# Accumulating gathers, rows that carry their weight, and another spread of the indexed transfers in a mixture-of-experts stage

## The chip, the core and the metric

The kernel runs on one core of one Trainium2 chip. The metric is the device time of one execution in microseconds. The core has five engines with a program each: PE (TensorE, matrix products into PSUM), DVE (VectorE), ACT (ScalarE), POOL (GpSimd) and SP (SyncE, which here only issues transfers). Engines wait for each other and for transfers by semaphores.

## The reference

The input x has four images of 32 x 128 x 128 in fp32. Each goes through two layers:

```
# layer 0: attention over the 4096 positions of an image folded 2 x 2
q = fold(x)                                  # 128 channels x 4096 positions
energy = q^T q / (norms)                     # in the reference's terms, d_i d_j
x = gamma * softmax(energy) applied to q + x
# layer 1: tokens t = 4096 rows of 128 per image
t = t + linear attention of layernorm(t)     # 8 heads; products collapse into one matrix
u = layernorm(t)
p, e = top 2 of softmax(u @ router_w + router_b), p normalised to sum 1
t = t + p0 * (u @ expert_w[e0] + expert_b[e0]) + p1 * (u @ expert_w[e1] + expert_b[e1])
```

What the change touches is the last line: for each token the results of its two experts are weighted and added.

## The kernel before

**Layer 0** (attend, line 416) runs image by image. One step of it makes one 128 x 512 block of scores: PE writes pe (line 550), ACT takes its exponential into pr (line 553; 531 in the last row of blocks of the last image) and PE multiplies pr with the values into po (line 439). Blocks are made once for the lower triangle; their transposes for the other triangle go by DVE (line 368), SP and DRAM (472, 487) into the tiles F, from which PE makes the share pg (line 374) at least 57 ticks of a clock of work later. There are 584 steps with an exponential in all, 144 an image and 8 more at the end.

**Everything else** is written as generators, which the loop at the end of the kernel advances by a piece each time the clock of work has moved by 10 (PACE), so about one piece a step. Instructions of PE, DVE, ACT and SP are issued in exactly the order in which these generators emit them. POOL's transfers by index and its powers are kept in program order too (pinned, line 158).

- prep (line 281) brings the next image's columns: loads xx, transposes it (ptq, 312), sums squares on DVE (323, 324), takes the power -0.5 on POOL (rn, 163), scales on DVE (qs, 337) and transposes again on PE (ptn, 345).
- layer1 (line 596) starts for an image when 84% of its steps are done, so most of it runs under the next image. close_rows(kc) closes one of four pieces of 8 rows of tokens: it divides (df, 703), adds to T (725), takes statistics (728), and sends them through close_stats to POOL's power (rsa, 163, and nba, 632). normalise (638) then writes xn, and gram_rows (670) adds to the gram matrix. After all four pieces comes matrix (764). Piece 0 of an image waits until the image before it has set "sorted" (line 686).
- attention_rows and route give each token its two experts, first and second, and their weights.
- sorted_experts(h) (line 914) handles one half h of an image's tokens, 16 rows of tiles. Each token gets two places in a list sorted by experts, one per expert. **32 scatters** on POOL (989) write the rows of xn to the DRAM list xs, one tile of 128 rows each. **Loads** (1015) bring the list back two tiles of one expert at a time, PE transposes them (1058) and multiplies with the expert's matrix (1051), DVE copies the product out (1034) and SP stores it in ys (1037). When all are done the second half sets "sorted". **32 gathers** on POOL (1116) then fetch for each tile of tokens the two results into yb; DVE multiplies them by their weights and adds them to acc (**combine**, 1085), which was fetched from t2 (1092), and SP stores four rows of acc to the output (**put**, 1098).

A scatter or gather waits for the latest exponential (exps), so that they are not issued faster than the steps go. Two are emitted a step. The scatters of half 1 wait in the program for those of half 0 ("moved"), the gathers of half 1 for those of half 0 ("gathered"), and those of half 0 for the scatters of half 1.

**The last image** has no image after it. Its close_rows run within its own last steps and after them; its last part (last_parts) does all experts for every token without sorting. Between the loop and last_parts the generators that are left are run to their end one after another, those of the earlier images first:

```
    for steps, _ in steady:
        for _ in steps:
            pass
    closing.last_parts()
```

## Time and profile before

| | us |
|---|---|
| runs | 1700.94, 1698.34, 1698.80 |
| median | 1698.8 |
| the profiled execution's own time | 1704.26 |
| its span | 1702.5 |
| mean granted TensorE clock | 0.993 |

In the table of groups each row is a line, engine and operation, with its count, busy time, mean length in ns, the idle time of the engine just before and what ended it. Groups that the change touches or that stand beside it:

```profile
L1116 POOL DMA_INDIRECT yb<-ys,place x192 | 185.3, 965 | 246.7 <-ACT pr L553 67.9
L989 POOL DMA_INDIRECT xs<-xn,place x192 | 185.8, 968 | 163.0 <-ACT pr L553 86.7
L384 DVE TENSOR_TENSOR o<-o,pg 128x512 f32<-128x512 f32 x110 | 75.4, 685 | 189.5 <-PE pg L374 156.2
L1034 DVE COPY xn<-pys 128x256 f32<-128x256 f32 x60 | 25.4, 424 | 89.2 <-ACT xn L1025 68.7
L1034 DVE COPY result<-pys 128x256 f32<-128x256 f32 (+1 forms) x60 | 24.6, 410 | 87.1 <-ACT xn L1025 57.8
```

The span falls into four images of about 400 us. The indexed transfers of an image run under the next image, so there are three such stages; the last image ends in a stretch of some 110 us without layer 0 beside it.

### The profile page before, as it was taken

The numbers are of one execution on the slowest core, as the hardware profiler recorded it, in microseconds if no ns is written. First come the engines' busy times: TensorE is split into PE (matmuls) and PEld (weight loads), VectorE is DVE, ScalarE is ACT, GpSimd is POOL, SyncE is SP. The second block draws the span as 40 slices with busy tenths as digits, with TensorE's granted clock in tenths as the row PEclk, the third lists the DMA queues.
The fourth block names the chain that finished last, engine by engine and source line by source line (L and its number), as shares of the span: only waits on it lengthen the run. The fifth ranks groups of instructions, "written<-read, shape, count | busy, mean of one in ns | idle before, by whom it ended". The sixth has DMA issues, their size and how long they took to land.

```text
span 1702.5 us, 21925 instructions
## 1 busy us (share of the span) xinstructions
PE 1651.5 (97%) x5458; PEld 876.1 (51%) x5458; DVE 936.7 (55%) x2443; ACT 926.0 (54%) x2893; POOL 511.0 (30%) x553
## 2 busy tenths in 40 slices
PE   8999999999999999999999999999999999998888
PEld 5444444455554555445554455545555455554643
DVE  4433334467485345478478334556748533454787
ACT  3555445466575555446565555545656455544476
POOL 1000000011026425451015642543102642446166
PEclk9999999999999999999999999999999999999999
DMA  4554756754458777875457777886445876876001
GB/s 135 168 177 157 204 173 219 242 190 162 149 173 266 229 239 243 255 225 161 136 179 235 228 248 240 236 258 194 165 141 167 264 228 216 254 243 193 7 12 39
DMA packets 227053, 325.51 MB, mean 191 GB/s; under 512 B 31472, under 2 KB 155504, under 8 KB 212592
## 3 DMA queue, kind: packets, MB, share of 16 engines
q1 hardware_dynamic: 206416, 285.15, 52.3%
q0 software_dynamic: 12288, 25.19, 5.1%
q10 hardware_dynamic: 8224, 13.77, 2.8%
q8 instruction: 46, 0.75, 0.2%
q14 instruction: 79, 0.65, 0.1%
HBM read 153.85 MB, written 175.24 MB: 193 GB/s over the span
## 4 chain that ended last, share of the span: by engine, by line
PE 79%; DVE 8%; DMA 4%; ACT 3%; issue 2%; SPq 2%; POOL 1%; another core or an unknown queue 0%; ACTq 0%; DVEq 0%; POOLq 0%
PE po L439 22%; PE pe L550 22%; PE pg L374 19%; PE pys L1051 3%; PE py L1200 3%; PE pg L395 2%; PE pys L1058 1%; PE pat L796 1%; ACT xn L638 1%; SPq L487 1%; DMA F<-blocks 1%; DVE df L703 1%; PE pgram L670 1%; PE ptq L312 1%; DMA blocks<-F 1%
## 5 line engine op out<-in xcount | busy, mean ns | idle before, releaser
L553 ACT ACTIVATE pr<-pe 128x512 f32<-128x512 f32 (+1 forms) x576 | 322.4, 560 | 552.0 <-PE pe L550 420.6
L439 PE MATMUL po<-pr,qT 128*128 128x512 f32 (+3 forms) x1152 | 551.9, 561 | 6.3 <-ACT o L444 5.6
L550 PE MATMUL pe<-qn,qn 128*128 128x512 f32 x896 | 462.5, 598 | 5.2 <-ACT pr L553 4.9
L374 PE MATMUL pg<-F,qT 128*128 128x512 f32 x880 | 451.1, 594 | 1.3 <-DMA F<-blocks 1.3
L368 DVE STREAM_TRANSPOSE F<-pr 128x512 f32<-128x512 f32 x440 | 305.8, 702 | 165.8 <-ACT pr L553 144.2
L439 PEld LDWEIGHTS po<-pr,qT 128*128 128x128 f32 x1152 | 216.0, 191 | 254.1 <-issue 223.7
L379 ACT ACTIVATE junk<-F 128x512 bf16<-128x512 f32 x440 | 272.9, 620 | 1.4 <-DMA F<-blocks 1.4
L374 PEld LDWEIGHTS pg<-F,qT 128*128 128x128 f32 x880 | 167.5, 191 | 197.2 <-issue 182.4
L1116 POOL DMA_INDIRECT yb<-ys,place x192 | 185.3, 965 | 246.7 <-ACT pr L553 67.9
L989 POOL DMA_INDIRECT xs<-xn,place x192 | 185.8, 968 | 163.0 <-ACT pr L553 86.7
L550 PEld LDWEIGHTS pe<-qn,qn 128*128 128x128 f32 x896 | 154.3, 192 | 114.7 <-issue 98.2
L384 DVE TENSOR_TENSOR o<-o,pg 128x512 f32<-128x512 f32 x110 | 75.4, 685 | 189.5 <-PE pg L374 156.2
L163 POOL TENSOR_TENSOR rn<-ss,neg_half 128x8 f32<-128x8 f32 (+1 forms) x17 | 26.9, 1584 | 332.6 <-DVE ss L324 332.5
L553 ACT ACTIVATION_READ_ACCUMULATOR pr<-pe 128x1 f32 x576 | 112.1, 195 | 0.0
L1025 ACT ACTIVATE xn<-pys 128x256 f32<-128x256 f32 x120 | 45.3, 378 | 109.8 <-PE pys L1058 87.5
L163 POOL TENSOR_TENSOR rsf<-dm_f,neg_half 128x8 f32<-128x8 f32 (+1 forms) x15 | 26.2, 1744 | 233.7 <-DVE sv_f L630 233.7
L1051 PEld LDWEIGHTS pys<-ew_sb,xn 128*128 128x128 f32 x468 | 69.6, 191 | 46.6 <-issue 43.8
L550 PE MATMUL pe<-qn 128*128 128x512 f32 (+3 forms) x256 | 90.4, 435 | 0.7 <-ACT qn L343 0.7
L379 ACT ACTIVATION_READ_ACCUMULATOR junk<-F 128x1 f32 x440 | 84.4, 192 | 0.0
L163 POOL TENSOR_TENSOR rsa<-dm_a,neg_half 128x8 f32<-128x8 f32 x16 | 26.5, 1654 | 186.5 <-DVE sv_a L630 186.2
L1034 DVE COPY xn<-pys 128x256 f32<-128x256 f32 x60 | 25.4, 424 | 89.2 <-ACT xn L1025 68.7
L1034 DVE COPY result<-pys 128x256 f32<-128x256 f32 (+1 forms) x60 | 24.6, 410 | 87.1 <-ACT xn L1025 57.8
(212 smaller groups left out, 1655.4 us busy)
## 6 DMA issues: line engine op xcount, KB each, us to landing
blocks<-F SPq DMA_DIRECT2D x110, 1024.0 KB
F<-blocks SPq DMA_DIRECT2D x220, 192.0 KB
F<-blocks SPq DMA_DIRECT2D x220, 128.0 KB
xn<-xs SPq DMA_DIRECT2D x114, 128.0 KB
F<-blocks SPq DMA_DIRECT2D x220, 64.0 KB
below<-F SPq DMA_DIRECT2D x31, 384.0 KB
out_dram<-acc SPq DMA_DIRECT2D x128, 64.0 KB
xx<-in_x_dram SPq DMA_DIRECT2D x62, 128.0 KB
```

What stands on the lines that cost most here:

```text
L163: pinned(nc.gpsimd.tensor_tensor(dst, src, neg_half.to_broadcast(list(src.shape)), ALU.pow))
L368: f()
L374: nc.tensor.matmul(pg.rearrange("p (a f) -> p a f", a=4), st["qT"][i][:, ib, :], G[:, :, ib], start=(ib == 0), stop=(ib == NJ - 1),)
L379: nc.scalar.activation(junk, G[:, :, ib], AF.Copy, accum_out=st["sums"][:, NJ * i + ib, jc : jc + 1])
L384: nc.vector.tensor_tensor(o, o, pg.rearrange("p (a j c) -> p a j c", a=4, c=S), ALU.add)
L439: nc.tensor.matmul(row["po"][:, lo:hi], qT[blk // NJ][:, blk % NJ, :], w, start=start, stop=(row["left"] == 0))
L550: nc.tensor.matmul(pe[:, c0:], qn[jc][:, ts(j, P)], qn[i][:, c0:], start=True, stop=True)
L553: nc.scalar.activation(pr[:, c0:], pe[:, c0:], AF.Exp, accum_out=sums[:, t, i : i + 1]).ins
L989: inst = nc.gpsimd.indirect_dma_start(xs[h], offset(place[:, i, k : k + 1]), xn[:, k, :], None)
L1051: nc.tensor.matmul(p[:, 2 * P + j * D : 2 * P + j * D + D], bufs[4 + g % 2][:, j, :], weights[:, bass.ds(begins[2 * (g % 2) + j], D)], sta ...
L1116: inst = nc.gpsimd.indirect_dma_start(yb[k // 4][:, i, k % 4, :], None, ys, offset(place[:, i, k : k + 1]))
L1200: nc.tensor.matmul(bank, xn[:, k, :], ew_sb[:, 4 * h : 4 * h + 4, :], start=True, stop=True)
```

## The change

- A row of the list xs is 132 numbers wide instead of 128 (DW = D + 4). Its last four hold the token's weight for that expert. POOL writes the weights into the same columns of xn before each run of 16 scatters; the scatters go through all rows of the half for the first expert and then for the second, instead of alternating. All other uses of xn name its first 128 columns.
- The product is multiplied on DVE by the weight that came with the row, instead of copied, into one of four buffers of the tile "df" (which close_rows uses too). Six buffers instead of four are loaded into.
- The gathers add in fp32 straight into acc, which is fetched first, so yb, combine and its 192 instructions on DVE are gone. In a group of four rows the gathers for the first expert come first, then those for the second, which add to the same bytes.
- The spread over steps: scatters have a free step after every four (for image 2 after every eight). Gathers go one a step for images 0 and 1, and for image 2 two a step with a free step after every four.
- place has two buffers instead of one.

```diff
-    xs = [dram.tile([NT * P, D], F32, tag=f"xs{h}", name=f"xs_{h}", bufs=1) for h in range(2)]
+    xs = [dram.tile([NT * P, DW], F32, tag=f"xs{h}", name=f"xs_{h}", bufs=1) for h in range(2)]
...
-        xn = big1.tile([P, KT, D], F32, tag="xn", name=f"xn_{b}")
+        xn = big1.tile([P, KT, DW], F32, tag="xn", name=f"xn_{b}")
...
-        place = stat.tile([P, 2, KT], U32, tag="place", name=f"place_{b}", bufs=1)
+        place = stat.tile([P, 2, KT], U32, tag="place", name=f"place_{b}")
...
             for n in range(2 * HR):
-                k, i = r0 + n // 2, n % 2
-                inst = nc.gpsimd.indirect_dma_start(xs[h], offset(place[:, i, k : k + 1]), xn[:, k, :], None)
+                i, k = n // HR, r0 + n % HR
+                if n % HR == 0:
+                    pinned(
+                        nc.gpsimd.tensor_copy(xn[:, half, D:], weight[:, i, half, :].to_broadcast([P, HR, DW - D]))
+                    )
+                inst = nc.gpsimd.indirect_dma_start(
+                    xs[h], offset(place[:, i, k : k + 1]), xn[:, k, :], None
+                )
...
                 if n % 2:
                     yield
                     yield
-                if h == 1 and n in (7, 15):
-                    yield from idle(2)
+                if n % 4 == 3 and (b < B - 2 or n % 8 == 7):
+                    yield from idle(1)
...
-                inst = nc.sync.dma_start(bufs[g % 4][:, :n], rows_of(xs[h], g, n))
+                inst = nc.sync.dma_start(bufs[g % 6][:, :n], rows_of(xs[h], g, n))
...
                     if applied:
                         g, n = applied
-                        if g % 4 < 2:
-                            result = bufs[6 + g % 2]
-                        else:
-                            result = work.tile([P, 2, D], F32, tag="grp", name=f"result_{b}_{h}_{g}", bufs=2)
-                        nc.vector.tensor_copy(
-                            result[:, :n], p[:, 2 * P : 2 * P + n * D].rearrange("p (j c) -> p j c", c=D)
+                        result = keep["results"][:, g % 4]
+                        nc.vector.tensor_tensor(
+                            result[:, :n], p[:, 2 * P : 2 * P + n * D].rearrange("p (j c) -> p j c", c=D),
+                            bufs[g % 6][:, :n, D : D + 1].to_broadcast([P, n, D]), ALU.mult,
                         )
...
+            if "results" not in keep:
+                keep["results"] = work.tile([P, 4, 2, D], F32, tag="df", name=f"results_{b}", bufs=1)
...
-                nc.vector.scalar_tensor_tensor(
-                    a[:, k % 4, :], yb[k // 4][:, i, k % 4, :], weight[:, i, k, :], a[:, k % 4, :], ALU.mult, ALU.add
-                )
...
-            for n in range(2 * HR):
-                k, i = r0 + n // 2, n % 2
...
-                inst = nc.gpsimd.indirect_dma_start(
-                    yb[k // 4][:, i, k % 4, :], None, ys, offset(place[:, i, k : k + 1])
-                )
-                wait_for(pinned(inst).ins, exps, "not more of these at a time than steps have")
-                after_steps.append((now[0] + 4, partial(combine, n)))
-                if n % 2:
-                    yield
-                    yield
-                    due()
+            groups = list(range(r0 // 4, (r0 + HR) // 4))
+            rate = 1 if b < B - 2 else 2
+            fetch(groups[0])
+            yield from idle(2)
+            for g in groups:
+                for n in range(8):
+                    i, k = n // 4, 4 * g + n % 4
+                    inst = nc.gpsimd.indirect_dma_start(
+                        accs[g][:, n % 4, :], None, ys, offset(place[:, i, k : k + 1]), compute_op=ALU.add
+                    )
+                    wait_for(pinned(inst).ins, exps, "not more of these at a time than steps have")
+                    if (n + 1) % rate == 0:
+                        yield
+                        yield
+                    if rate == 2 and n % 4 == 3:
+                        yield from idle(1)
+                    if n == 3 and g != groups[0]:
+                        put(g - 1)
+                    if n == 3 and g != groups[-1]:
+                        fetch(g + 1)
             turns[h].append("gathered")
-            while after_steps:
-                yield
-                yield
-                due()
-            yield
+            yield from idle(4)
+            put(groups[-1])
             yield
```

## The prediction

> **What bounds the kernel now.** I read the page's busy table first, then busy time by stretches of 60 us, then the waits of PE, then the timelines of DVE and POOL where PE lost time, and last the chain of waits in order of time.
>
> ```profile
> PE 1651.5 (97%) x5458; PEld 876.1 (51%) x5458; DVE 936.7 (55%) x2443; ACT 926.0 (54%) x2893; POOL 511.0 (30%) x553
> ```
>
> PE is the bound. It is idle for 51 us of the span, so what DVE no longer has to do is worth something only where PE waits for DVE. The stretches (length; then PE, PEld, DVE, ACT and POOL busy; granted clock; DMA share; GB/s) show where:
>
> ```profile
> 660.00:720.00 60.00, 60.00 (x211) 32.60 (x210) 32.23 (x76) 32.15 (x99) 28.86 (x31) 1.00 0.82 247
> 720.00:780.00 60.00, 54.21 (x159) 27.04 (x158) 42.87 (x117) 28.54 (x91) 30.05 (x30) 0.94 0.73 219
> 1140.00:1200.00 60.00, 56.16 (x182) 30.00 (x181) 45.86 (x129) 32.39 (x105) 21.13 (x21) 0.94 0.61 193
> 1600.00:1620.00 20.00, 16.68 (x128) 14.89 (x127) 12.11 (x43) 5.43 (x13) 1.84 (x2) 1.00 0.00 1
> ```
>
> After the start and before the end PE loses time mainly where one image hands over to the next (5.8 us from 720 to 780, 3.8 us from 1140 to 1200). In 660 to 720, full of gathers and weighted additions, it loses none. The first hand-over in the timelines of PE, then DVE (start, length, idle before in brackets):
>
> ```profile
> 723.41 0.72 PE L312 MATMUL ptq<-ident,xx 128*128 128x128 f32 x4 [2.06 <-DMA xx<-in_x_dram]
> ...
> 747.84 0.91 PE L345 MATMUL ptn<-ident,qs 128*128 128x128 f32 x4 [3.07 <-issue]
> 748.54 1.92 PE L550 MATMUL pe<-qn,qn 128*128 128x512 f32 x2
> 750.25 1.65 PE L439 MATMUL po<-pr,qT 128*128 128x512 f32 x2
> ```
>
> ```profile
> 739.66 2.78 DVE L703 TENSOR_TENSOR df<-o,pbd 64x512 f32<-64x512 f32 x4
> 742.47 0.71 DVE L368 STREAM_TRANSPOSE F<-pr 128x512 f32<-128x512 f32 x1
> 743.11 0.69 DVE L1085 SCALAR_TENSOR_TENSOR acc<-yb,weight,acc 128x128 f32<-128x128 f32 x2
> 743.72 1.22 DVE L725 TENSOR_TENSOR T<-T,df 128x1024 f32<-128x1024 f32 x1
> 744.97 0.87 DVE L728 BATCH_NORM_STATS2 bs_a<-T 128x6 f32<-128x128 f32 x4
> ...
> 747.10 1.28 DVE L337 TENSOR_TENSOR qs<-qT,rn 128x512 f32<-128x512 f32 x2
> ```
>
> The 3.07 us has "issue" beside it, but ptn starts at 747.84, just after the first of the two qs (747.10 plus half of 1.28): PE waits for DVE, which has close_rows' division, addition and statistics in front of qs. The same 3.07 us stands at 1151.75.
>
> The third place is the end, where the last image's four pieces are closed. Timeline of POOL:
>
> ```profile
> 1572.41 0.94 POOL L1116 DMA_INDIRECT yb<-ys,place  x1 [0.30 <-issue]
> 1585.86 1.77 POOL L163 TENSOR_TENSOR rsa<-dm_a,neg_half 128x8 f32<-128x8 f32 x1 [12.50 <-DVE sv_a L630]
> 1593.90 1.64 POOL L163 TENSOR_TENSOR rsa<-dm_a,neg_half 128x8 f32<-128x8 f32 x1 [5.99 <-DVE sv_a L630]
> 1605.78 1.64 POOL L163 TENSOR_TENSOR rsa<-dm_a,neg_half 128x8 f32<-128x8 f32 x1 [9.96 <-DVE sv_a L630]
> ```
>
> and the chain of waits (start, length, what), which goes through the last of these:
>
> ```profile
> 1604.02 0.80 DVE bs_a L728 x4
> 1605.78 1.64 POOL rsa L163
> 1608.27 2.07 PE pgram L670 x16
> 1610.70 2.10 PE pgv L781 x6
> ```
>
> Today POOL issues its last gather at 1572.41 and is free for each rsa. After rsa come the normalisation, gram and the matrix, and nothing fills PE meanwhile. A microsecond that the fourth rsa is late is a microsecond of the kernel.
>
> **What the Trainium skill says.** "TensorE: Matmul & The Clock Gate", the table at its head: GpSimd's queue is strictly first in, first out; so an rsa stands behind every gather issued before it. The timeline agrees (gathers and rsa never overlap). The same page, Part 1, has an idle PE drop to half rate and need some 3.4 us of work to recover; here the two pairs after the 3.07 us wait take 1.71 and 1.49 us from start to start instead of 0.86. "DMA: Bandwidth & Descriptors", Rules for kernel authors: an accumulating DMA must wait for the semaphore of an earlier one on the same bytes; the kernel before has none, so no run shows it yet. The section on the SWDGE path there gives about 2 us of fixed cost, mostly completion.
>
> **Part by part: the middle.** 192 weighted additions leave DVE; two take 0.61 to 0.65 us from start to start, so 192 x 0.32 = 61 us of 936.7. Nearly all of it lies beside PE. The result's copy (L1034, 410 to 424 ns) becomes a multiply of the same shape from PSUM; L384 does twice the elements in 685 ns, so I cost it at nothing, hidden under PE; 10% more would be 60 x 2 x 0.04 = 5 us of DVE, again beside PE.
>
> Order matters more. One step is one exponential (584 in all), so step n is the n-th L553 or L531 in ACT's timeline. With the slower scatters "sorted" is set at step 282 instead of 270 for image 0 (426 instead of 414 for image 1; 562 instead of 558 for image 2). In the built program close_rows of the next image then stands behind qs on DVE. In front of qs, since its sums, are two transposes, one addition and two results: 2 x 0.63 + 0.61 + 2 x 0.42 = 2.7 us, against 747.10 - 739.66 = 7.4 us. The 4.7 us exceed 3.07, so both ptn waits go, with the recovery: 2 x (3.07 + (1.71 - 0.86) + (1.49 - 0.86)) = 9.1 us. What is late next: pieces 0 and 1 of close_rows now begin 3 steps apart rather than 8, so DVE is full for some 13 us; this can cost PE 0 to 3 us a hand-over; I take 0.75 each, 1.5. The waits for xx (2.06 and 1.52 us) stay: SP carries results and tiles there as before. If they go too, with recovery, some 6 us more is gained; if the stretched stage makes them worse, 3 us is lost.
>
> Tiles of 132 instead of 128 columns add 3% of bytes in scatters and loads, and rows that no longer start on 512 B; accumulating gathers read their destination too. The DMA share is 0.83 at most (1080 to 1140), and PE's waits for F are 1.7 us in the whole span, so I cost this at nothing; if the slack behind F went, a few us. The 12 weight copies on POOL are small and POOL is idle there. Ahead of the second in each half POOL waits for 16 scatters to land, with one rn behind it at most: nothing. Fetches on ACT's queue and stores on SP's wait for gathers issued 3 to 4 steps (8 to 11 us) earlier: no wait taken.
>
> **The end.** A half's gathers of image 2 are stretched over some 29 steps. Those of half 0 run from step 540 to 569; those of half 1 start at 569 (1552.46 us in ACT's timeline), and the loop ends at 586. What is left is issued in one go, ahead of the close of the last piece. In the built program POOL's queue reads: ten gathers, second rsa, two gathers, third rsa, twenty gathers, fourth rsa. Back to back a gather takes 0.94 + 0.30 = 1.25 us.
>
> Without combines DVE is up to 1.3 us earlier for the third rsa, so 1592.7; with nba done at 1594.7; twenty gathers take 25.0, and the fourth rsa starts at 1619.7 instead of 1605.78: +13.9. If DVE gained 3 us more, 10.2 would be the least (second rsa 1584.5, 1.9, two gathers 2.5). Accumulating gathers on POOL: not below 0.95, as they name the same rows; if the destination as a second source makes it half as much again (estimate 1.43), twenty add 10 us. I take 0.95 as the nearest row. The fifth gather of a group waits for the first, issued 5.0 us earlier; with the 2 us of the page it has landed; at 6 us it would cost 1 to 2 us in each of three groups. PE's 36 fillers end at 1606.7, so PE goes cold for 15 us: gram, gv and the matrix (2.05 + 2.10 + 2.02) lose 0 to 5; I take 2.
>
> Sum: -9.1 + 1.5 + 13.9 + 2 = +8.3 us. The profiled execution took 1704.26 (span 1702.5), 5.5 above the median of 1698.8; so the span becomes about 1710.8 and the median 1707.
>
> **Rivals.** (1) Dearer accumulation: 1.43 us a gather, or late landings: 10 us more, 1717. For it: every gather now depends on another; against: no row shows more than 0.97. (2) Relief of DVE outweighs: the xx waits go too (9.1 + 6 = 15) and the third rsa comes 3 us early, so the end costs 10.2 with PE soon warm: -5, 1694. It decides once the hand-overs return more than the fourth rsa's delay. For it: DVE is the releaser in both places; against: xx waits for DMA, not DVE. (3) The two balance: within 3.4 us of 1698.8.
>
> **How the numbers follow.** My forecast 0.56 (own range 1702 to 1713), dearer accumulation 0.20, balance 0.12, relief 0.12. No change that can be told is 0.2%, 3.4 us. Slower 0.76, same 0.12, faster 0.12. The range reaches from just inside the balance, 1698, to a little past rival 1, 1720.
>
> **What would show it.** Right: no 3.07 us wait at ptn in the second and third hand-over, twenty gathers between the third and fourth rsa, the fourth rsa 14 us later against the third than now (25 instead of 11.9), with POOL and not DVE in front of it in the chain, and PE idle there. Wrong: a gather of POOL over 1.2 us, new waits of PE for F or xx in the product stages, or a fourth rsa that still waits for DVE.

## The result: slower, and where the profile shows it

| | before | changed |
|---|---|---|
| median of five runs each, us | 1698.34 | 1708.0 |
| all runs, us | 1697.02 to 1700.94 | 1706.19 to 1709.41 |
| ratio, 95% interval | | 1.0059 (1.0046 to 1.0071) |
| the profiled execution: span, us | 1702.5 | 1706.2 |

The profiled execution of the changed kernel lies on its median; that of the kernel before (1704.26) lay 5.9 us above its own. Lines of the changed kernel carry numbers that are 1 higher up to the sorting, and differ by up to 9 after it: the gathers are now L1107, the scatters L994, the powers L164.

The page of the changed kernel, its first part, and two of its groups (count, busy us, mean ns of one, idle before):

```profile
PE 1645.4 (96%) x5458; PEld 876.4 (51%) x5458; DVE 880.4 (52%) x2251; ACT 927.5 (54%) x2893; POOL 630.9 (37%) x565
...
L1107 POOL DMA_INDIRECT acc<-ys,place x192 | 301.9, 1572 | 304.7 <-ACT pr L554 198.3
L994 POOL DMA_INDIRECT xs<-xn,place x192 | 185.6, 967 | 196.7 <-ACT pr L554 123.6
```

DVE lost 56 us and POOL gained 120. Of the 120, 117 are the 192 gathers: 1572 ns each instead of 965. The scatters still take 967. The queue of these transfers holds 33792 packets instead of 12288; the difference, 21504, is 192 times 112, so a gather of 128 rows went from 32 packets to 144.

Busy time by stretches, the changed kernel (columns as before):

```profile
720.00:780.00 60.00, 59.09 (x212) 32.63 (x211) 38.45 (x99) 35.09 (x108) 32.20 (x22) 1.00 0.75 205
1140.00:1200.00 60.00, 59.30 (x217) 33.77 (x216) 44.55 (x123) 38.08 (x122) 29.59 (x21) 1.00 0.62 173
1580.00:1600.00 20.00, 0.00 (x0) 0.00 (x0) 0.00 (x0) 0.00 (x0) 16.65 (x12) 0.60 0.41 62
1600.00:1620.00 20.00, 9.66 (x49) 8.29 (x50) 3.39 (x10) 2.64 (x6) 7.99 (x6) 0.63 0.19 30
```

The hand-overs are repaired: PE is busy for 59.1 and 59.3 us of 60 instead of 54.2 and 56.2. More than that is lost in 1580 to 1600, where PE, DVE and ACT do nothing at all and POOL alone works, and the granted clock falls to 0.60.

POOL's timeline there (the rows left out are sixteen more gathers and one nba), and PE's (start, length, idle before):

```profile
1567.11 1.67 POOL L164 TENSOR_TENSOR rsa<-dm_a,neg_half 128x8 f32<-128x8 f32 x1
...
1569.56 1.64 POOL L1107 DMA_INDIRECT acc<-ys,place  x1 [0.50 <-issue]
1571.50 1.55 POOL L1107 DMA_INDIRECT acc<-ys,place  x1 [0.30 <-issue]
...
1603.61 1.54 POOL L1107 DMA_INDIRECT acc<-ys,place  x1 [0.30 <-issue]
1605.45 1.54 POOL L1107 DMA_INDIRECT acc<-ys,place  x1 [0.30 <-issue]
1606.43 2.27 POOL L164 TENSOR_TENSOR rsa<-dm_a,neg_half 128x8 f32<-128x8 f32 x1
```

```profile
1575.81 4.15 PE L186 MATMUL spare<-ident 128*128 128x128 f32 x36 [0.25 <-ACT xnT L657]
1609.57 3.78 PE L671 MATMUL pgram<-xn 128*128 128x128 f32 x16 [29.61 <-ACT xn L639]
```

Twenty gathers stand between the third rsa and the fourth. From start to start they take 1.84 us, in all 36.9 us from 1569.56 to 1606.43. The releaser that PE's row names, ACT's xn, is only the last link: xn waited for nba, nba for rsa, and rsa for the gathers. The chain of waits (start, length, what) runs through the same place:

```profile
1571.50 1.55 POOL acc L1107
...
1606.99 1.72 POOL rsa L164
1609.57 3.79 PE pgram L671 x16
1613.73 2.59 PE pgv L782 x6
```

To lay the two executions beside each other I use the steps (one exponential each) and the fourth rsa as marks:

| us | before, first profile | before, second profile | changed |
|---|---|---|---|
| step 340 | 906.34 | 904.80 | 899.35 |
| step 484 | 1311.70 | 1310.01 | 1297.48 |
| step 536 | 1454.39 | 1450.45 | 1434.05 |
| step 584, the last | 1591.72 | 1585.19 | 1566.03 |
| from there to the fourth rsa | 14.06 | 14.07 | 40.40 |
| from the fourth rsa to the end of the span | 96.7 | 95.5 | 99.8 |

The second profile of before is the first experiment. Against it the changed kernel is 19.2 us ahead at the last step, gives back 26.3 up to the fourth rsa and 4.3 after it: +11.4, which is the distance of the two spans (1706.2 and 1694.8). Against the first profile the lead is 25.7, the distance 3.7; so 6.5 us of that lead belonged to one execution of the kernel before. At step 536 the changed kernel has also put some of its work off, so that its lead there is partly order; this is counted below.

### The profile page after: what moved, and what is told of

It is laid out like the page before. It is cut to its first block, busy times and chain, and to the rows that moved or that the text cites. A ratio compares the mean times of both kernels' runs of the same rounds, so it can differ in the third digit from the quotient of the medians.

```text
span 1706.2 us, 21751 instructions
## 1 busy us (share of the span) xinstructions
PE 1645.4 (96%) x5458; PEld 876.4 (51%) x5458; DVE 880.4 (52%) x2251; ACT 927.5 (54%) x2893; POOL 630.9 (37%) x565
## 3 DMA queue, kind: packets, MB, share of 16 engines
q0 software_dynamic: 33792, 25.58, 8.5%
## 4 chain that ended last, share of the span: by engine, by line
PE 81%; DVE 7%; ACT 4%; POOL 3%; DMA 2%; issue 2%; SPq 1%; ACTq 0%; DVEq 0%; POOLq 0%
PE po L440 23%; PE pe L551 22%; PE pg L375 19%; PE pys L1056 3%; PE py L1192 2%; PE pg L396 2%; POOL acc L1107 2%; PE pys L1063 1%; ACT xn L639 1%; PE pgram L671 1%; PE pat L797 1%; DVE df L704 1%; PE ptq L313 1%; ACT pr L554 1%; DVE F L369 1%
## 5 line engine op out<-in xcount | busy, mean ns | idle before, releaser
L1107 POOL DMA_INDIRECT acc<-ys,place x192 | 301.9, 1572 | 304.7 <-ACT pr L554 198.3
L994 POOL DMA_INDIRECT xs<-xn,place x192 | 185.6, 967 | 196.7 <-ACT pr L554 123.6
L1038 DVE TENSOR_TENSOR results<-pys,xn 128x256 f32<-128x256 f32 x120 | 50.1, 417 | 190.6 <-ACT xn L1032 151.7
L164 POOL TENSOR_TENSOR rn<-ss,neg_half 128x8 f32<-128x8 f32 (+1 forms) x17 | 26.9, 1582 | 321.2 <-DVE ss L325 321.2
L639 ACT ACTIVATE xn<-T,nba,rsa 128x128 f32<-128x128 f32 x120 | 49.2, 483 | 43.5 <-POOL nba L633 43.5
L1056 PE MATMUL pys<-ew_sb,xn 128*128 x468 | 71.6, 275 | 0.0
L164 POOL TENSOR_TENSOR rsa<-dm_a,neg_half 128x8 f32<-128x8 f32 x16 | 30.1, 1881 | 112.0 <-DVE sv_a L631 111.7
```

The costliest lines, as they stand in the source:

```text
L164: pinned(nc.gpsimd.tensor_tensor(dst, src, neg_half.to_broadcast(list(src.shape)), ALU.pow))
L639: nc.scalar.activation(xn[:, k, :D], T[:, k, :], AF.Identity, scale=rs[:, k, :], bias=nb[:, k, :])
L994: inst = nc.gpsimd.indirect_dma_start(xs[h], offset(place[:, i, k : k + 1]), xn[:, k, :], None)
L1056: nc.tensor.matmul(p[:, 2 * P + j * D : 2 * P + j * D + D], bufs[6 + g % 2][:, j, :D], weights[:, bass.ds(begins[2 * (g % 2) + j], D)], st ...
L1107: inst = nc.gpsimd.indirect_dma_start(accs[g][:, n % 4, :], None, ys, offset(place[:, i, k : k + 1]), compute_op=ALU.add)
```

## The experiments

Two questions were open: what makes the end so dear, and what gives the lead in the middle. The kernel before was run again with each batch; ratios are to these runs. Its median differed from batch to batch (1699.84, 1700.51, 1705.14, 1691.34), so times of different batches are compared through the marks of their profiles, not directly.

### The kernel before, once more

No edit.

> A second profile of the kernel before, to see which waits of the first belong to the program and which to that one execution. If the two 3.07 us waits at ptn and the two waits for xx are the program's, they stand again within 0.5 us; the 2.33 us wait of PE at ptd (line 465, 1575.13) named nothing that the order of the program explains, so I expect it to be gone or elsewhere. If the gain of the changed kernel up to the last step (25.7 us earlier at step 584) is partly that execution's, this profile reaches step 584 some 3 to 6 us earlier than 1591.7.

Measured: 1696.6 (one run, span 1694.8), before 1699.84; so this profile is of an execution 3.2 us quicker than the median. The waits at ptn stand again (3.09 us each), and those for xx (2.00 and 2.72 us, the second 1.2 us longer than in the first profile). The wait at ptd, which was expected to go, stands too, with 1.84 us. Step 584 comes 6.5 us earlier, a little more than expected; the marks are those of the table above. What the first profile had in excess was spread over many places; nothing of it is used below.

### The end: gathers that don't add

```diff
-    accs[g][:, n % 4, :], None, ys, offset(place[:, i, k : k + 1]), compute_op=ALU.add
+    accs[g][:, n % 4, :], None, ys, offset(place[:, i, k : k + 1])
```

The addition is left out: a gather overwrites acc.

> The changed kernel with plain gathers instead of accumulating ones: the addition is left out (the later gather overwrites), all waits and places in the queues stay. Theory A (what an accumulating gather costs POOL makes the end long): a gather falls from 1.55 to about 0.95 us busy, 1.25 from start to start; the twenty gathers between the third and the fourth rsa take 25 instead of 37 us, the wait of PE before the last gram falls from 29.6 to about 18 us, the time from 1708 to about 1696 (1693 to 1699). Theory B (gathers wait for the landing of those on the same bytes, the busy time is only what is seen of that): gathers stay at about 1.5 us, time 1706 to 1710.

Measured: 1691.02 (1690.72 to 1691.32), ratio 0.9949 (0.9929 to 0.9969). POOL's timeline, around the same twenty gathers:

```profile
1589.38 0.94 POOL L1107 DMA_INDIRECT acc<-ys,place  x1 [0.30 <-issue]
1590.63 0.94 POOL L1107 DMA_INDIRECT acc<-ys,place  x1 [0.30 <-issue]
1591.60 1.68 POOL L164 TENSOR_TENSOR rsa<-dm_a,neg_half 128x8 f32<-128x8 f32 x1
```

A gather starts every 1.25 us again, and the packets are 12288. The fourth rsa stands 28.3 us behind the last step (1563.27) instead of 40.4. So the accumulation costs POOL 0.59 us a gather, 11.8 us for the twenty; the spans are 16.8 us apart, more than the 12 expected, since the last step comes 2.8 us earlier and the stage after the rsa takes 2.0 us less. Theory B falls: the waits and places stayed, and the busy time went. Nor does it look like a wait for room behind the gather before: of the changed kernel's 192 gathers, the 34 that found POOL idle for more than 2 us have a median of 1.54 us, like the 73 that came within 0.4 us of what was before them. What POOL does in the added time, the traces don't tell. The Trainium skill, "DMA: Bandwidth & Descriptors", section "SWDGE vs HWDGE vs iDMA", says that descriptors of this path are computed by software on a GpSimd core and that only this path can accumulate. It gives no price for it. The traces fit this: more packets (144 a gather instead of 32) and longer POOL instructions appear and vanish together.

### The end: no free steps in image 2

```diff
                     if (n + 1) % rate == 0:
                         yield
                         yield
-                    if rate == 2 and n % 4 == 3:
-                        yield from idle(1)
```

> The changed kernel with the free steps between the gathers of image 2 taken out, so that all 64 are issued before the loop ends and none stands between the third and fourth rsa. Theory A (their place ahead of the fourth rsa is what costs): the last wait of PE for normalise falls from 29.6 to under 8 us; POOL then needs 3.7 us for two gathers in a step of 2.6 us and falls behind, which gives part of it back at the first rsa or at puts on SP; time 1683 to 1694. Theory B (the end costs the same wherever the gathers stand, as POOL has the same work): 1704 to 1710.

Measured: 1695.78 (1694.09 to 1697.87), just above what theory A gave, ratio 0.9975 (0.9967 to 0.9984). Two gathers instead of twenty stand between the third rsa (1582.57) and the fourth (1595.72), which waits for DVE again (6.60 us). But step 584 comes at 1577.35, 11.3 us later than in the changed kernel. POOL's timeline inside the loop shows why: from 1529 to 1587 POOL has no pause above 0.5 us, and the first two rsa, at 1540.89 and 1573.23, stand in the middle of it. PE waits for what hangs on them (start, length, idle before):

```profile
1544.03 2.08 PE L671 MATMUL pgram<-xn 128*128 128x128 f32 x8 [4.43 <-ACT xn L639]
1576.34 1.64 PE L671 MATMUL pgram<-xn 128*128 128x128 f32 x8 [1.20 <-ACT xn L639]
```

In the changed kernel PE has no wait above 0.25 us from 1520 us to the last step. The free steps do not merely delay the gathers; they keep POOL from holding up the last steps. What they put off has to be paid in the drain.

### The end: the last image first

```diff
-    for steps, _ in steady:
+    for steps, _ in reversed(steady):
         for _ in steps:
             pass
     closing.last_parts()
```

> The changed kernel with one thing turned round: after the last step, what is left of image 3's first part is handed out before what is left of image 2's gathers. Two of the twenty late gathers then stand ahead of the fourth rsa, eighteen behind it and ahead of the first rsf. Theory A (each accumulating gather holds POOL for 1.84 us, and what stands behind the rest is late): the fourth rsa at 1577 to 1583 us instead of 1606.43, the gram matmuls within 4 us of it; the first rsf, ready some 15 us later, is held until eighteen gathers of 1.84 us have passed, 1612 to 1616 instead of 1623.78; 1695 to 1701 in all. Rival N (the twenty gathers only fill a hole, the end is set by something else of the last image): 1705 to 1710.

Measured: 1696.69 (1695.47 to 1698.20), ratio 0.9979 (0.9971 to 0.9987). POOL's timeline (seventeen gathers, and nba, left out):

```profile
1578.89 1.67 POOL L164 TENSOR_TENSOR rsa<-dm_a,neg_half 128x8 f32<-128x8 f32 x1 [6.02 <-DVE sv_a L631]
...
1612.93 1.55 POOL L1107 DMA_INDIRECT acc<-ys,place  x1 [0.30 <-issue]
1613.92 2.26 POOL L164 TENSOR_TENSOR rsf<-dm_f,neg_half 128x8 f32<-128x8 f32 x1
```

As theory A had it. The fourth rsa is 27.5 us earlier and waits for DVE, not POOL; the gram matmuls start at 1581.42. The eighteen gathers then stand in front of the next power, the first rsf, which is only 9.9 us earlier than before this edit, and the span is 11.7 shorter. The same gathers cost less here, since the first 12 us or so of them lie beside other work: the rsf would not have been ready until 14.5 us after the rsa, by the second profile of before (1599.26 to 1613.74).

### The middle: the new spread alone, in the kernel before

```diff
-        place = stat.tile([P, 2, KT], U32, tag="place", name=f"place_{b}", bufs=1)
+        place = stat.tile([P, 2, KT], U32, tag="place", name=f"place_{b}")
...
-                if h == 1 and n in (7, 15):
-                    yield from idle(2)
+                if n % 4 == 3 and (b < B - 2 or n % 8 == 7):
+                    yield from idle(1)
...
-                if n % 2:
+                if n % 2 or b < B - 2:
                     yield
                     yield
                     due()
```

The second hunk is the scatters' spacing, the third the gathers' (one a step for images 0 and 1). Gathers don't add, and all 192 additions stay on DVE.

> The kernel before with only the new spread: free steps between scatters, one gather a step for images 0 and 1, two buffers of place; rows of 128, yb and the 192 weighted additions on DVE stay. Theory S (the later 'sorted' puts close_rows behind qs, and the spread thins the transfers; the additions on DVE cost nothing): the waits at ptn and xx go, 7 us for each of two hand-overs, time about 1685 (1682 to 1689). Theory D (the additions' removal from DVE is what shortened the hand-overs): at least half of the waits stay, 1692 to 1699.

Measured: 1687.71 (1685.92 to 1688.73), ratio 0.9928 (0.9912 to 0.9944). This is faster than both kernels. Step 484 comes at 1298.95 and step 536 at 1435.11, 11.1 and 15.3 us ahead of the kernel before (second profile), where the changed kernel has 12.5 and 16.4. So nearly all of the lead up to there is the spread's. The waits of PE from 500 to 1500 us (us in total, how many, longest), first of the kernel before (second profile), then of this one:

```profile
PE ptq L312 <- DMA xx<-in_x_dram: 4.7, 2, 2.7
PE ptn L345 <- DVE o L384: 3.1, 1, 3.1
PE ptn L345 <- DVE qs L337: 3.1, 1, 3.1
PE pe L550 <- ACT pr L553: 3.0, 6, 0.9
```

```profile
PE pe L550 <- ACT pr L553: 1.4, 2, 0.7
PE pbd L716 <- DVE rdx L694: 1.4, 2, 0.7
PE pys L1058 <- DMA xn<-xs: 1.0, 1, 1.0
```

Both kinds of wait are gone, for DVE and for the load of xx. For ptn the order is what the prediction had: in DVE's timeline of the changed kernel qs now comes before the division of close_rows, where in the kernel before it came behind it.

```profile
738.02 1.29 DVE L338 TENSOR_TENSOR qs<-qT,rn 128x512 f32<-128x512 f32 x2
746.67 2.81 DVE L704 TENSOR_TENSOR df<-o,pbd 64x512 f32<-64x512 f32 x4 [3.73 <-PE pbd L717]
```

It is the same in every run with the new spacing of the scatters, and in none with the old.

### The middle: the additions left out of the kernel before

```diff
-                a = accs[k // 4]
-                nc.vector.scalar_tensor_tensor(
-                    a[:, k % 4, :], yb[k // 4][:, i, k % 4, :], weight[:, i, k, :], a[:, k % 4, :], ALU.mult, ALU.add
-                )
```

> The kernel before with VectorE's 192 additions left out (the gathers stay as they are, two a step into yb, which nothing reads; the experts' results are not added). Theory B (bursts of VectorE's additions at the hand-overs make the waits at ptn and xx): those waits are gone or under 1.4 us, step 340 at 901 to 903 us, step 484 at 1300 to 1305, 1688 to 1694 in all. Rival P (the waits come from where POOL's gathers and the experts' part fall in the order): ptn waits of some 3 us stand at both hand-overs, step 340 at 904 to 906, 1695 to 1699.

Measured: 1696.68 (1692.75 to 1702.72), ratio 0.9950 (0.9938 to 0.9963), before 1705.14. The same waits of PE:

```profile
PE pe L550 <- ACT pr L553: 7.9, 6, 3.1
PE ptq L312 <- DMA xx<-in_x_dram: 5.0, 2, 2.7
...
PE ptn L345 <- issue: 0.6, 2, 0.3
```

Neither theory holds whole. The waits at ptn do go, as theory B says (6.2 to 0.6 us). But waits for pr come in their place (3.0 to 7.9), one of 3.07 us 20 us after the place of the old one, and xx stays. Step 340 comes at 904.34 and step 484 at 1306.94, 0.5 and 3.1 us earlier than in the kernel before: rival P's value for step 340, and above B's range for step 484. The time lies in P's range too, but the kernel before stood at 1705.14 in this batch, and the ratio is half a per cent below 1. In the profiled executions, taking 58 us of work off DVE (936.0 to 878.1) was worth 3.3 us at step 536 and 1.7 us at step 584; the runs, with more scatter than most, give more, up to 8 us. Which of the two is nearer is not settled.

### The middle: scatters' spacing alone, gathers' spacing alone

The kernel before with the second hunk of the spread alone, and with its first and third hunk alone:

```diff
-                if h == 1 and n in (7, 15):
-                    yield from idle(2)
+                if n % 4 == 3 and (b < B - 2 or n % 8 == 7):
+                    yield from idle(1)
```

> The kernel before with only the new spacing of the scatters; its gathers stay at two a step, the additions stay on VectorE. Theory S1 (the scatters' spacing carries the gain): step 240 near 611 us (before 616.86), step 340 at 900 to 902, step 484 at 1299 to 1302, and 1686 to 1691 in all. Rival S2 (the gathers' spacing carries it): step 340 at 904 to 906, step 484 at 1308 to 1312, and 1695 to 1699.

```diff
-        place = stat.tile([P, 2, KT], U32, tag="place", name=f"place_{b}", bufs=1)
+        place = stat.tile([P, 2, KT], U32, tag="place", name=f"place_{b}")
...
-                if n % 2:
+                if n % 2 or b < B - 2:
```

> The kernel before with only the new spacing of the gathers of images 0 and 1 (one a step, two buffers of places); the scatters stay as they were. Theory S1: step 340 at 904 to 906 us, step 484 at 1308 to 1312, and 1695 to 1699 in all. Rival S2: step 340 at 900 to 902, step 484 at 1299 to 1302, and 1686 to 1691. A share for each would show as step 340 near 903 and a time near 1693.

Measured, in one batch with before at 1700.51: scatters alone 1695.77 (1692.17 to 1698.37), ratio 0.9970 (0.9958 to 0.9982); gathers alone 1688.45 (1687.43 to 1689.68), ratio 0.9923 (0.9908 to 0.9939). How far each is ahead of the second profile of before, in us:

| step | additions left out | scatters alone | gathers alone | both | changed kernel |
|---|---|---|---|---|---|
| 240 | -1.0 | 5.7 | 1.0 | 6.1 | 5.7 |
| 288 | -0.3 | 9.9 | 8.6 | 9.2 | 10.3 |
| 340 | 0.5 | 3.3 | 3.4 | 4.2 | 5.5 |
| 484 | 3.1 | 7.0 | 10.9 | 11.1 | 12.5 |
| 536 | 3.3 | 10.9 | 12.4 | 15.3 | 16.4 |
| 584 | 1.7 | 7.3 | 8.1 | 10.9 | 19.2 |

With the scatters' new spacing, the rows of steps 240, 288 and 536 do not compare equal work. By step 240 PE has done 86 of the 234 matmuls of image 0's experts (tile pys) in the kernel before, and only 38 where the scatters, and so the products, come later. The view for pys alone, from 480 us to step 240 (length; then PE's busy time and count, and the rest as before), of the kernel before in its second profile and of the scatters alone:

```profile
480.00:616.88 136.88, 11.94 (x86) 11.06 (x86) 5.95 (x14) 5.73 (x15) 1.00 0.75 235
480.00:611.19 131.19, 5.34 (x38) 4.93 (x38) 2.55 (x6) 2.69 (x7) 1.00 0.71 222
```

The missing products are 6.6 us of PE, so the 5.7 us at step 240 are work put off, not a gain, although S1 had the value right. By step 536 it is 104 matmuls against 125, some 3 us; at step 288 it is sixteen gram matmuls. At steps 340, 484 and 584 every row has done the products of the images before.

At equal work, then, either spacing alone gives 3.3 or 3.4 us by step 340 and both together 4.2; by step 484 the scatters' gives 7.0, the gathers' 10.9 and both 11.1. The two don't add up, and the gathers' spacing alone gives nearly all. The medians say the same: 4.7 and 12.1 us below before. By time S2 holds: the gathers' spacing alone reaches what both reach, and the scatters' stays in S2's range, though its profiled execution was at the quick end of its runs, so that its row is flattered. With scatters alone no wait at ptn or xx above 0.4 us is left, but PE waits at gram for xn instead (5.3 us in four waits from 500 to 1500 us); with gathers alone 1.4 us is left at each ptn and none at xx.

### The middle: the changed kernel with the old scatters

```diff
-                if n % 4 == 3 and (b < B - 2 or n % 8 == 7):
-                    yield from idle(1)
+                if h == 1 and n in (7, 15):
+                    yield from idle(2)
```

> The changed kernel with the scatters' old spacing (no free step but the two pauses in the second half), so that the experts' part of each image starts some 12 steps earlier, as before; the accumulating gathers and the missing additions stay. Theory S (the gain of the middle comes from where the order puts the experts' part, not from VectorE's 192 missing additions): step 340 is reached near 905 us (after: 899.35; before, second execution: 904.80), step 484 near 1308 (after 1297.48), the waits for ptn or xx of 2 to 3 us stand again, and the time is 1713 to 1720. Rival D (VectorE's relief takes the waits away): step 340 by 901, step 484 by 1300, and 1705 to 1710 in all.

Measured: 1705.26 (1703.64 to 1709.85), ratio 1.0025 (1.0013 to 1.0036). Theory S missed: the waits of 2 to 3 us at ptn and xx don't come back, and steps 340 and 484 come at 902.32 and 1303.27, between the two theories; the time lies in rival D's range. D's reason isn't shown by that: the gathers' spacing, which stayed, removes the waits for xx with all additions in place too. PE's waits from 500 to 1500 us now are

```profile
PE pe L551 <- ACT pr L554: 9.4, 5, 3.2
PE po L440 <- ACT o L445: 1.7, 6, 0.5
PE ptn L346 <- issue: 0.6, 2, 0.3
```

The first are waits of 2 to 3 us under the scatters themselves (the largest begin at 548, 951 and 1350). At step 240 this kernel is 3.5 us behind the kernel before (620.36 against 616.88), with the same spacing of the scatters, as many products done and no gather issued yet. So something else in the change costs there at the old spacing, the wider rows or the order of the scatters perhaps; no run separates it.

The last step comes at 1576.78, 10.7 us later than in the changed kernel, and the fourth rsa still at 1606.69, against 1606.43. The gathers of image 2 begin earlier in the order, and fourteen, not twenty, are left behind the third rsa: that rsa is 11.6 us later, and six gathers fewer are 11.0 us. The two shifts cancel, so that ten microseconds of the middle made no difference to the fourth rsa: POOL's queue set it.

### Attempts at a better kernel

**Free steps for image 2 as well, with additions on DVE.** The spread alone, and

```diff
+                if b == B - 2 and n % 4 == 3:
+                    yield from idle(1)
```

> The kernel of the run that spreads alone (additions on VectorE, plain gathers), and in image 2 also a free step after every four gathers, as the changed kernel has them. Theory: what that run lost to the changed kernel between steps 554 and 584 (37.6 and 48.3 us for the two parts against 34.3 and 44.5) comes from two gathers a step; step 584 then at 1566 to 1570 us instead of 1574.25; more plain gathers (1.25 us each) are left for the drain, where POOL had 11 us free ahead of the fourth rsa; 1683 to 1689 in all. Rival: the loss comes from the additions on VectorE themselves; step 584 stays at 1573 to 1576, the left-over gathers hold the fourth rsa, and 1688 to 1695.

Measured: 1696.51 (1695.63 to 1697.11), ratio 0.9947 (0.9934 to 0.9960), before 1705.14; above both ranges. The first half of the theory holds: step 584 comes at 1567.41, so the 8 us that the spread alone lost to the changed kernel there were lost to two gathers a step, not to the additions. The second half fails. PE's timeline:

```profile
1591.26 1.12 PE L643 MATMUL ptx<-ident,xn 128*128 128x128 f32 x4 [17.23 <-DVE gram L666]
```

DVE's shows what held gram: twelve additions, each waiting for its own gather, stand in front of it (start, length, idle before; the first and the last two, and gram):

```profile
1577.04 0.35 DVE L1085 SCALAR_TENSOR_TENSOR acc<-yb,weight,acc 128x128 f32<-128x128 f32 x1 [1.12 <-DMA yb<-ys,place]
...
1589.34 0.35 DVE L1085 SCALAR_TENSOR_TENSOR acc<-yb,weight,acc 128x128 f32<-128x128 f32 x1 [0.86 <-DMA yb<-ys,place]
1590.65 0.35 DVE L1085 SCALAR_TENSOR_TENSOR acc<-yb,weight,acc 128x128 f32<-128x128 f32 x1 [0.96 <-DMA yb<-ys,place]
1590.92 0.67 DVE L666 TENSOR_TENSOR gram<-gram,pgram 128x128 f32<-128x128 f32 x2
```

**The changed kernel with its late gathers where POOL waits.** The last image's last_parts gets the generators left of image 2 as older; gathers(n) advances them by n gathers:

```diff
-    for steps, _ in steady:
-        for _ in steps:
-            pass
-    closing.last_parts()
+    for _ in steady[-1][0]:
+        pass
+    closing.last_parts(steady[-2][0])
...
-            for _ in matrix():
-                pass
+            for at, _ in enumerate(matrix()):
+                if at % 2 == 0 and at < 6:
+                    gathers(2)
...
             stats_of(1)
+            gathers(12)
             attended(2)
```

> The changed kernel with the late gathers of image 2 put where POOL waits: two ahead of the fourth rsa, six ahead of the first rsf, twelve behind the second rsf. Theory A (an accumulating gather costs POOL 1.84 us and nothing else, and only the powers that stand behind it make it dear): fourth rsa at 1577 to 1581 us, first rsf at 1592 to 1596, the first sum of rows some 9 us later against the rsf than in the other kernels; 1680 to 1687 in all. Rival C (accumulating transfers also cost the last image through the queues or POOL's last stage, which has little slack): 1689 to 1696.

Measured: 1692.68 (1692.46 to 1693.53), ratio 0.9926 (0.9913 to 0.9940), before 1705.14. The powers come as theory A has them: fourth rsa 1579.62, first rsf 1594.14. The time is in the rival's range, and its second half, that POOL's last stage has little slack, is what the trace shows. DVE's timeline at the place that decides:

```profile
1635.35 0.35 DVE L1136 SCALAR_TENSOR_TENSOR acc<-py,first,T 128x128 f32<-128x128 f32 x1 [14.68 <-POOL nbf L633]
```

There is one more power, the third rsf (16 columns wide), and it starts only at 1632.07, behind the twelve gathers and the first two sums of rows, which start at 1623.39. PE stands 10.8 us for the tiles that hang on it. So the rule was right and the list of powers incomplete; theory A had counted two.

**Plain gathers, spread to the last, put where POOL waits.** The kernel with free steps for image 2 and the same way of handing out; eight gathers go between the fourth rsa and the first rsf, four behind the second:

```diff
-            gv = work.tile([P, NH, D + E], F32, tag="wide", name=f"gv_{b}")
+            gv = (fpool.tile([P, NH, D + E], F32, tag="F", name=f"gv_{b}") if alone else work.tile([P, NH, D + E], F32, tag="wide", name=f"gv_{b}"))
...
-            for _ in matrix():
-                pass
+            for at, _ in enumerate(matrix()):
+                if at % 2 == 0:
+                    gathers(2)
...
             stats_of(1)
+            gathers(4)
             attended(2)
+            gathers(2)
             attended(3)
+            for _ in older:
+                pass
```

> A version that is to beat both kernels: the one with spread alone and free steps in image 2 as well (plain gathers, additions on VectorE), with its late gathers put where POOL waits: eight between the fourth rsa and the first rsf, four behind the second rsf; the last image's gv has a buffer of its own for this. Theory A (only what stands behind the late gathers makes them dear, and plain ones of 1.25 us fit into POOL's idle stretches of 12 and 11 us): step 584 near 1567 us, fourth rsa at 1579 to 1582, first rsf at 1593 to 1597, the last stage as long as in the spread alone (81 us from the rsf to the end); 1677 to 1684 in all, a ratio of 0.986 to 0.990. Rival V (the additions that wait for them on VectorE now stand in the way of the last image's own work there): first rsf after 1598 or a last stage of over 85 us, 1685 to 1692, a ratio over 0.990.

Measured: 1688.79 (1687.49 to 1689.71), ratio 0.9986 (0.9978 to 0.9994), before 1691.34. Step 584 comes at 1566.71, the fourth rsa at 1580.42 and the first rsf at 1595.01, all as theory A has them, and the last stage takes 91.5 us from there instead of 81. Rival V names it. DVE's timeline:

```profile
1598.69 2.69 DVE L1085 SCALAR_TENSOR_TENSOR acc<-yb,weight,acc 128x128 f32<-128x128 f32 x8
1604.05 0.35 DVE L1085 SCALAR_TENSOR_TENSOR acc<-yb,weight,acc 128x128 f32<-128x128 f32 x1 [2.67 <-DMA yb<-ys,place]
...
1608.14 0.28 DVE L808 TENSOR_TENSOR lw<-nba,srw 128x128 f32<-128x128 f32 x1
```

From 1598.69 to 1608.14 DVE adds and waits for image 2 while the routing of the last image stands behind it; PE's wait for the tiles of that routing is 11.74 us. No version is shown to beat the spread alone: it took 1687.71, the gathers' spacing alone 1688.45, this one 1688.79 and the changed kernel with its late gathers moved 1692.68. The ratios are 0.9928, 0.9923, 0.9986 and 0.9926, but each is to the kernel before in its own batch, which moved by more than these differ.

## Why the prediction was right in its time and wrong in its terms

The forecast of 1707 met 1708.0. The mechanism of the end was the one named; its price was short by half, and the middle gave more than it was credited with. The two errors have opposite signs and nearly the same size, so that the sum came out to 1 us is luck. So is the sign: with gathers at the price that the forecast gave them the kernel is faster than before, not slower (the run without the addition, ratio 0.9949). One of the prediction's own signs of being wrong came true: a gather of POOL over 1.2 us.

| term, us | predicted | against the first profile of before | against the second |
|---|---|---|---|
| the middle, up to the last step | -9.1 + 1.5 = -7.6 | -25.7 | -19.2 |
| last step to fourth rsa | +13.9 | +26.3 | +26.3 |
| after the fourth rsa (cold PE) | +2 | +3.1 | +4.3 |
| sum | +8.3 | +3.7 | +11.4 |

The medians differ by 9.7.

**Gathers ahead of the fourth rsa: right in place and number, wrong in price.** Twenty gathers, from the built order, stood where the prediction put them, POOL and not DVE came before the rsa in the chain, and PE idled. The step that failed is "I take 0.95 as the nearest row". A gather that adds keeps POOL for 1.57 us and starts every 1.84, so twenty take 36.9 us instead of 25.0. That is 11.9 of the 12.4 us by which the term was short. The run without the addition reproduces the step as it was worked out: 28.3 us from the last step to the fourth rsa, against 14.06 + 13.9 = 28.0. The doubt was held as the first rival (1.43 us, 1717), with "no row shows more than 0.97" against it; but no row of an accumulating gather existed, so that was no evidence. Its price was the nearer one, and its time was still wrong, because the middle gained more.

**The middle up to step 484: the wait at ptn as predicted, the waits for xx not.** The ptn waits went, and in the changed kernel by the order that the prediction read from the built program: qs at 738.02, the division at 746.67. That is one way of several: leaving out the additions alone, or spacing the gathers alone with "sorted" where it was (the last product's result comes at step 268; 269 in the kernel before, 282 in the changed one), shrinks them to 0.3 and 1.4 us. The step "The waits for xx (2.06 and 1.52 us) stay: SP carries results and tiles there as before" failed; no run with the gathers' or the scatters' new spacing has them, and the run without additions has. The prediction said what that would be worth: "some 6 us more". Added to the rest, this makes 9.1 - 1.5 + 6 = 13.6 us for the hand-overs, and the changed kernel is 12.5 ahead at step 484, where no work is put off. DVE's relief was held to be beside PE, and the profile of before without additions agrees with that: 3.1 us ahead at step 484, 1.7 at step 584.

**The last 100 steps: a term that the prediction doesn't have.** From step 484 to 584 the changed kernel goes from 12.5 to 19.2 us ahead. What decides there is the free step after every four gathers of image 2. With it the spread with plain gathers goes from 10.7 to 17.8. Without it the spread alone goes from 11.1 to 10.9, and the changed kernel from 12.6 to 7.8. So these free steps are what makes the last steps quick, and what leaves twenty gathers for the end; the prediction saw only the second. The 11.6 us by which the middle was short are therefore 4.9 up to step 484, where the waits for xx went (4.7 us in the second profile of before), and 6.7 behind it.

**The new burst on DVE was priced a little too high (1.5):** two waits of 0.43 us for rdx at pbd, and waits of 0.25 to 0.46 us for xn at gram, are what is left at the hand-overs.

**Cold PE: 2 predicted.** gram, gv and the matrix took 3.79, 2.59 and 1.87 us in the chain, 2.2 more than the sum of 2.07, 2.10 and 1.87 in that of before. The rest of the 3.1 is mostly the rsa's record, 2.27 instead of 1.64 us: it begins 0.56 us before that of the last gather ends (1605.45 + 1.54), so this part belongs to the gathers.

**Landings, wider rows, DVE's multiply: nothing, as costed, in the changed kernel.** The multiply takes 417 ns, the copies 410 and 424. PE has no wait for F above 0.2 us from 500 to 1500. At the old spacing of the scatters something there did cost, 3.5 us by step 240, as shown above.

**The relief rival named 1694 and fell, as did the balance (within 3.4 us of 1698.8),** although the condition of the first came true: the xx waits went and DVE was ahead. It said that this decides "once the hand-overs return more than the fourth rsa's delay". Up to the last step 19.2 were returned, 12.5 of them by step 484, against 26.3. With gathers that don't add, that would have been enough: 1691 against 1699.84.

What stays open is how the spacing of the transfers removes the waits for xx: POOL is busy for 23 instead of 30 us of 720 to 780 in the spread alone, and the transfers, the products and the hand-over's own work fall in other steps, but no run separates these.

## What to carry to other kernels

Moving work off an engine that isn't the bound is worth what its waits are worth, and a wait that is removed can come back at the next reader, as it did at pr without the additions and at gram with the scatters' spacing alone. How evenly indexed transfers are handed out was worth more here than 192 instructions saved (11.1 against 3.1 us at step 484). Two kernels compare at a mark only if both have done the same work by then; a lead of 5.7 us at step 240 was products put off. Work put off to a drain must be priced at the in-order queue where it ends up, with every instruction behind it listed: here each of three powers in turn became the one that the late gathers held. When the unknown price multiplies a count on the path (twenty gathers), take the dearer end of the bound, for no row of another operation speaks against it.

## What the runs showed of the hardware that was not expected

- A gather of 128 rows of 512 B by index that adds in fp32 takes POOL 1572 ns instead of 965, and starts every 1.84 us instead of 1.25; its packets go from 32 to 144. A scatter of rows of 528 B took 967 ns, no more than one of 512 B (968).
- In the changed kernel 13 records on POOL begin up to 0.58 us before the record of the accumulating gather ahead of them ends, as the fourth rsa does. With plain gathers, in both profiles of before and in the run without the addition, none does. Whether work overlaps there the records don't tell.
- The kernel before had a median of 1691.34 in one batch and 1705.14 in another, while the marks of the kernels with the spread agreed across batches: step 536 came at 1435.11, 1435.44 and 1434.73 in three of them, in three batches. It may be that the order with waits at its hand-overs is also the less repeatable one. But the batches ran on different chips, and medians are compared with single profiles here; no run was made to test it.
